# A copy of the centred rows between TensorE and the norm, in the attention layers of a four-layer graph network

## The chip, the cores and the metric

The kernel runs on one core of one Trainium2 chip. The metric is the device time of one execution in microseconds. A profile is one more execution of the same program, recorded by the hardware profiler; its span is the time from its first to its last instruction. Engines are named as in the profile: PE is the matrix engine (PEld its weight loads), DVE the vector engine, ACT the scalar engine, POOL GpSimd, SP the engine that issues most transfers.

## The reference

Input is x, of shape (8, 2048, 128), and a 2048 x 2048 adjacency matrix that is sparse (some 17 neighbours a row). Four layers follow one another: attention, graph, attention, graph. An attention layer is a transformer block whose softmax runs over a node's neighbours alone, with 8 heads of 16; a graph layer has one additive score for each edge. Cut to what matters:

```python
# attention layer (0 and 2)
scores = einsum('bnhd,bmhd->bhnm', h @ Wq, h @ Wk) / sqrt(16)      # by heads
attn = softmax(where(adj == 0, -inf, scores))
x = h + (attn @ (h @ Wv) @ Wo + bo)
x = layer_norm(x) * ln1_g + ln1_b
y = relu(x @ W1 + b1) @ W2 + b2                                    # 128 -> 256 -> 128
x = layer_norm(x + y) * ln2_g + ln2_b
# graph layer (1 and 3)
h = x @ W
e = leaky_relu((h @ a_src)[:, :, None] + (h @ a_dst)[:, None, :], 0.2)
out = softmax(where(adj == 0, -inf, e)) @ h
x = ln_gamma * layer_norm(out + x) + ln_beta
```

The layer norm is (x - mean) / sqrt(variance + 1e-5) over the 128 features. It stands twice in each attention layer and once in each graph layer; the change is in the two of the attention layers.

## The kernel before

**Units.** The 2048 nodes are cut into 32 units of 64. Batches come in two halves of four, so a unit's data is a tile of 128 partitions (64 nodes by two halves) by 4 x 128 columns; transposed it is 128 features by 512. At the start the kernel builds, from the adjacency, the list of neighbour rows that each unit needs (`block_list`, `unit_list`), as nine groups of 128 rows. Building runs alongside layer 0. Each layer then reads a table in HBM that the layer before wrote (`project`, its copies into the tile `trows`).

**An attention unit.** For each unit `attention` takes five steps: four of two groups and one of a single group. A step gathers rows of keys and values by indirect DMA from POOL's queue (`kv<-table,idx`, L1469), PE spreads the queries over them (`qe`, L1542), DVE multiplies (L1554) and reduces over a head's 16 columns (`s`, L1561), ACT takes the exponential (L1571), POOL weighs the values (L1580; for some steps DVE does, from an exponential that ACT puts into a PSUM tile `ps_e`), and PE sums by target node (`acc` and `sums`, L1615). The buffer `kv` exists six times.

**After attention.** `after_attention` takes the sums of a unit: DVE divides (L1633, L1637), PE transposes (`ps_t`), ACT copies to `at`, PE multiplies by Wo (`ps_o`), DVE adds bias and residual into the tile `r` (L1649). Then comes the norm. `centred` multiplies `r` by I - 1/128 on PE, which takes the mean off and turns the rows back, into the PSUM tile `ps_c` (L1310). `norm` reads it twice: four squares with their sum (ACT, L1406, each followed by a read of the accumulator), a root as logarithm and exponential (L1416, L1417), and four scalings by it into `normed` (L1439). `scaled` transposes (`ps_t`, L1298) and applies gain and offset (L1449). Two products with W1, the rectifier into `hidden` (L1669), a product with W2 (`ps_y`, L1679), the second sum into another `r`, and the second norm in the same manner follow; at the end the rows go to HBM (`xd`) and into the next layer's table (L1345 or L1343, L1288, L1383).

**The graph layers** use the same `norm`. There `r` is an SBUF tile that DVE wrote (L1865: `ps_c` plus the weighted sum), so both readings are from SBUF.

**What sets the order.** Every operation is given to a planner with a cost for each engine that may run it, a key, the cells that it reads and writes, and the buffers that it takes. `Plan.order` is a list scheduler: at each moment an engine takes the ready operation of the smallest key whose buffers are free. Its result is the program order of each engine, and each engine then runs in that order. A unit's steps have keys from n x 1000 + 5u on; its exponentials come four earlier and its norm five later. So the exponential of a step goes ahead of the norms when both are ready, but doesn't interrupt one that runs. `either` lets ACT alone run an operation, and ACT or DVE in the last two units of a layer (`late`):

```python
def either(self, scalar, vector):
    return {"ACT": scalar, "DVE": vector} if self.late else {"ACT": scalar}
```

**Buffers that bear on the change.** All small PSUM tiles (`ps_q`, `ps_t`, `ps_o`, `ps_c`, `ps_f`, `ps_y`, `ps_p`, `ps_e`, and those of the list building: `ps_off`, `ps_aux`, `ps_l`) share the tag `m` with two slots. `r` has two buffers in SBUF.

```python
PSUM_BUFS = {"q": 1, "acc": 1, "sums": 1, "m": 2}
```

The functions that the diff touches, with what calls them:

Of the kernel before, what the change touches and what calls it, by code (L numbers as in the profile page):

```python
# [65 lines left out]
class Dense:  # L66
# [181 lines left out]
    def norm(self, out, r, gain, offset):  # L248

        nc = self.nc  # L250
        stats = self.two.tile([P, TB, 6], F32, name="stats")
        mv = self.two.tile([P, TB, 2], F32, name="mv")
        for t in range(TB):
            nc.vector.bn_stats(stats[:, t, :], r[:, t, :])
        for t in range(TB):
            nc.vector.bn_aggr(mv[:, t, :], stats[:, t, :])
        ve = self.two.tile([P, TB], F32, name="ve")
        nc.gpsimd.tensor_scalar(ve, mv[:, :, 1], EPS, None, ALU.add)
        rstd = self.two.tile([P, TB], F32, name="rstd")
        nc.gpsimd.tensor_tensor(rstd, ve, self.neg_half, ALU.pow)  # L260
        xn = self.one.tile([P, TB, P], F32, name="xn")
        for t in range(TB):
            nc.vector.tensor_scalar(
                xn[:, t, :], r[:, t, :], mv[:, t, 0:1], rstd[:, t : t + 1], ALU.subtract, ALU.mult
            )
        nc.gpsimd.tensor_tensor(xn, xn, gain.unsqueeze(1).to_broadcast([P, TB, P]), ALU.mult)
        nc.gpsimd.tensor_tensor(out, xn, offset.unsqueeze(1).to_broadcast([P, TB, P]), ALU.add)
# [146 lines left out]
    def after_attention(self, x, L, c, heads):  # L414

        nc = self.nc
        x = x[:, c * TB : (c + 1) * TB, :]
        ft = self.across(heads)
        ps = self.ps_m.tile([P, CH], F32, name="ps_p", tag="m")
        for t in range(TB):  # L420
            cols = slice(t * P, (t + 1) * P)
            nc.tensor.matmul(ps[:, cols], lhsT=ft[:, cols], rhs=L["Wo"], start=True, stop=True)
        r = self.one.tile([P, TB, P], F32, name="r")
        nc.vector.tensor_tensor(r, ps.rearrange("p (t e) -> p t e", t=TB), x, ALU.add)
        x1 = self.one.tile([P, TB, P], F32, name="x1")
        self.norm(x1, r, L["ln1_g"], L["ln1_b"])
        ft = self.across(x1)
        nc.gpsimd.tensor_tensor(x1, x1, L["b2"].unsqueeze(1).to_broadcast([P, TB, P]), ALU.add)
        hidden = self.one.tile([P, FFN // P, CH], F32, name="hidden")
        for f in range(FFN // P):  # L430
            ps = self.ps_m.tile([P, CH], F32, name="ps_f", tag="m")
            nc.tensor.matmul(ps, lhsT=L["W1"][:, f * P : (f + 1) * P], rhs=ft, start=True, stop=True)
            nc.scalar.activation(hidden[:, f, :], ps, AF.Relu, bias=L["b1"][:, f : f + 1])
        ps = self.ps_m.tile([P, CH], F32, name="ps_y", tag="m")
        for t in range(TB):
            cols = slice(t * P, (t + 1) * P)
            for f in range(FFN // P):
                nc.tensor.matmul(
                    ps[:, cols],
                    lhsT=hidden[:, f, cols],  # L440
                    rhs=L["W2"][:, f, :],
                    start=(f == 0),
                    stop=(f == FFN // P - 1),
                )
        r = self.one.tile([P, TB, P], F32, name="r")
        nc.vector.tensor_tensor(r, ps.rearrange("p (t e) -> p t e", t=TB), x1, ALU.add)
        self.norm(x, r, L["ln2_g"], L["ln2_b"])
# [290 lines left out]
def flat(ap):  # L738
    return ap if len(ap.shape) == 2 else ap.rearrange("p b d -> p (b d)")


class Sparse:
# [585 lines left out]
    def project(self, n, u, x, key, of=None, shares=()):  # L1328
# [66 lines left out]
            {"SP": 0.9}, store, key, reads=[rows], joins=[self.table[n]], dma=P * hb * width * 4  # L1395
        )

    def norm(self, r, key):

        hb = self.HB  # L1400
        var = self.cell("var", [P, hb, 2])

        def squares(e, b):
            x = flat(r.tile)[:, b * P : (b + 1) * P]
            if e is self.nc.scalar:
                e.activation(self.junk, x, AF.Square, scale=P**-0.5, accum_out=var.tile[:, b, 1:2])  # L1406
            else:
                e.bn_stats(self.stats, x)
                e.bn_aggr(var.tile[:, b, :], self.stats)

        for b in range(hb):
            self.op(self.either(0.55, 0.4), lambda e, b=b: squares(e, b), key, reads=[r], joins=[var])
        rstd = self.cell("rstd", [P, hb])

        def root(e):
            e.activation(rstd.tile, var.tile[:, :, 1], AF.Ln, bias=self.eps)  # L1416
            e.activation(rstd.tile, rstd.tile, AF.Exp, scale=-0.5)  # L1417

        self.op({"ACT": 0.5}, root, key - 2, reads=[var], writes=[rstd])
        normed = self.cell("normed", [P, hb, P])  # L1420
        for b in range(hb):
            self.op(
                self.either(0.37, 0.28),
                lambda e, b=b: self.scale(
                    e, normed.tile[:, b, :], flat(r.tile)[:, b * P : (b + 1) * P], rstd.tile[:, b : b + 1]
                ),
                key,
                reads=[r, rstd],
                joins=[normed],
            )  # L1430
        return normed
# [194 lines left out]
    def after_attention(self, n, u, acc, sums, x, base):  # L1626
        self.late = u >= self.NU - 2
        L, hb = self.layers[n], self.HB
        op, cell = self.op, self.cell
        key = base + TG  # L1630
        rc = cell("rc", [P, hb * H])

        op({"DVE": 0.35}, lambda e: e.reciprocal(rc.tile, sums.tile), base, reads=[sums], writes=[rc])  # L1633
        a = cell("rows", [P, hb, P], name="a")

        def divide(e):
            e.tensor_tensor(  # L1637
                a.tile.rearrange("p b (h d) -> p (b h) d", d=HD),
                acc.tile.rearrange("p (c d) -> p c d", d=HD),
                rc.tile.unsqueeze(2).to_broadcast([P, hb * H, HD]),  # L1640
                ALU.mult,
            )

        op({"DVE": 0.65}, divide, base, reads=[acc, rc], writes=[a])

        def add_to(r, ps, bias, other, key):
            op(
                {"DVE": 0.72},
                lambda e: e.scalar_tensor_tensor(r.tile, ps.tile, bias, other.tile, ALU.add, ALU.add),  # L1649
                key,  # L1650
                reads=[ps, other],
                writes=[r],
            )

        at = cell("at", [P, CH])
        ps = self.transposed(a, key, at)
        op(self.either(0.6, 0.68), lambda e, ps=ps: self.copy(e, at.tile, ps.tile), key, reads=[ps], writes=[at])
        r = cell("r", [P, CH], name="r1")
        ps = self.product(L["Wo"], at, key, "ps_o", r)
        add_to(r, ps, L["bo"], x, key - 2)  # L1660
        normed = self.norm(self.centred(r, key), key)
        x1 = self.scaled(normed, L["ln1_g"], L["ln1_b"], "x1", key)
        hidden = cell("hidden", [P, FFN // P, CH])
        for f in range(FFN // P):
            ps = self.product(L["W1"][:, f * P : (f + 1) * P], x1, key, "ps_f", hidden)

            def relu(e, f=f, ps=ps):
                if e is self.nc.scalar:
                    e.activation(hidden.tile[:, f, :], ps.tile, AF.Relu, bias=L["b1"][:, f : f + 1])  # L1669
                else:  # L1670
                    e.tensor_scalar(hidden.tile[:, f, :], ps.tile, L["b1"][:, f : f + 1], 0.0, ALU.add, ALU.max)

            op(self.either(0.7, 0.68), relu, key, reads=[ps], joins=[hidden])
        r = cell("r", [P, CH], name="r2")
        ps = cell("m", [P, CH], name="ps_y")
        for f in range(FFN // P):
            op(
                {"PE": 1.0},
                lambda e, f=f, ps=ps: e.matmul(  # L1679
                    ps.tile,  # L1680
                    lhsT=L["W2"][:, f, :],
                    rhs=hidden.tile[:, f, :],
                    start=(f == 0),
                    stop=(f == FFN // P - 1),
                ),
                key,
                reads=[hidden],
                writes=[ps],
                holds=[r],
            )  # L1690
        add_to(r, ps, L["b2"], x1, key - 2)
        normed = self.norm(self.centred(r, key), key)
        x = self.scaled(normed, L["ln2_g"], L["ln2_b"], "xnew", key)
        self.keep(u, x, key)
        self.project(n + 1, u, x, key)
# [297 lines left out]
```

## Time and profile before

| | us |
|---|---|
| median of three runs | 3263.28 |
| the three runs | 3248.80, 3263.28, 3274.68 |
| the profiled execution | 3296.99 |
| its span | 3295.2 |

| engine | busy us | share of the span |
|---|---|---|
| PE | 2532.1 | 77% |
| DVE | 2311.1 | 70% |
| ACT | 1399.5 | 42% |
| POOL | 2104.5 | 64% |

The stages, by the places in the trace where POOL stops gathering: attention 0 up to about 1190 us (the lists to 850), graph 1 to about 1790, attention 2 to about 2720, graph 3 to the end. The span holds 63,421 instructions and moves 1023 MB, 310 GB/s on the mean, with a granted TensorE clock of 0.867. A share of busy time over the whole span mixes these stages; a stage's own share is read from the table of windows.

A row of a group reads: line, engine, operation, output and inputs by tile, partitions x elements of output and input, count; behind the bar the busy time in us and the mean ns of one; behind the second bar the idle time of the engine just before these instructions, and what ended it. A row of waits reads: who waited, for whom, us in total, times, the longest. A row of the timeline reads: start, duration, engine, line, operation.

### The profile page before, as it was taken

How to read it: one execution, taken by the hardware profiler on the slowest of the kernel's cores; microseconds unless marked ns; L12 is line 12 of the kernel's file. 1: busy time of each engine (PE TensorE's matmuls, PEld its weight loads, DVE VectorE, ACT ScalarE, POOL GpSimd, SP SyncE). 2: the span in 40 equal slices, each digit the busy share in tenths (PEclk: the TensorE clock that was granted, in tenths of full speed). 3: DMA queues.
4: the chain of work that ended last, by engine and by line, in shares of the span. 5: the costliest groups of instructions: out<-in, count | busy, mean ns of one | idle time of the engine just before them, and what ended most of it. 6: DMA issues, size and time to landing. Idle time of an engine off the chain costs nothing. (4 is left out here: it accounts for less than half of the span.)

```text
span 3295.2 us, 63421 instructions
## 1 busy us (share of the span) xinstructions
PE 2532.1 (77%) x23624; PEld 1474.1 (45%) x23624; DVE 2311.1 (70%) x3617; ACT 1399.5 (42%) x4894; POOL 2104.5 (64%) x1447
## 2 busy tenths in 40 slices
PE   6777888878878866788876788888887785777675
PEld 5633444444334334565654233334443343555454
DVE  4789889878878763444444998998989873445554
ACT  4435455555444422444443244444444441333333
POOL 0168777777878835555563777878787835555552
PEclk8769889899999977888898899999999996778877
DMA  7868879887889749999997989999998848899994
GB/s 252 304 228 325 313 285 370 308 337 292 321 321 347 301 156 322 347 327 332 324 352 257 358 331 376 356 353 350 357 354 351 352 186 281 289 317 313 312 302 160
DMA packets 261246, 1023.15 MB, mean 310 GB/s; under 512 B 40193, under 2 KB 69633, under 8 KB 189025
## 3 DMA queue, kind: packets, MB, share of 16 engines
q0 software_dynamic: 166464, 864.44, 70.4%
q1 hardware_dynamic: 94464, 154.56, 13.7%
q8 instruction: 190, 3.11, 0.4%
q14 instruction: 128, 1.04, 0.1%
HBM read 978.59 MB, written 88.08 MB: 324 GB/s over the span
## 5 line engine op out<-in xcount | busy, mean ns | idle before, releaser
L1469 POOL DMA_INDIRECT kv<-table,idx x1152 | 1191.3, 1034 | 931.7 <-issue 395.9
L1580 POOL TENSOR_TENSOR kv<-kv 128x2048 f32<-128x2048 f32 (+1 forms) x252 | 900.0, 3584 | 76.8 <-ACT kv L1571 72.9
L1554 DVE TENSOR_TENSOR kv<-qe,kv 128x2048 f32<-128x2048 f32 (+1 forms) x320 | 662.7, 2071 | 184.6 <-DMA kv<-table,idx 117.2
L1561 DVE TENSOR_REDUCE s<-kv 128x128 f32<-128x2048 f32 (+1 forms) x320 | 659.4, 2061 | 11.4
L1542 PE MATMUL qe<-q_sb,hot 32*128 32x512 f32 (+1 forms) x2304 | 400.2, 700 | 193.7 <-DVE kv L1554 183.5
L1615 PE MATMUL acc<-kv,hot 128*32 128x512 f32 x2560 | 371.4, 658 | 55.1 <-POOL kv L1580 49.6
L1810 DVE TENSOR_TENSOR w<-hot,e 128x512 f32<-128x512 f32 (+1 forms) x384 | 222.2, 597 | 163.6 <-ACT e L1800 83.0
L1825 PE MATMUL acc_q<-kv,w 128*32 128x129 f32 x5120 | 264.7, 314 | 93.7 <-issue 66.7
L1825 PE MATMUL acc<-kv,w 128*32 128x129 f32 x2560 | 155.1, 330 | 135.2 <-issue 89.1
L1825 PEld LDWEIGHTS acc_q<-kv,w 128*32 128x32 f32 x5120 | 177.3, 124 | 166.7 <-issue 117.5
L1542 PEld LDWEIGHTS qe<-q_sb,hot 32*128 32x128 f32 (+1 forms) x2304 | 106.7, 197 | 319.3 <-DVE kv L1554 247.8
L1571 ACT ACTIVATE kv<-s 128x128 f32<-128x128 f32 (+1 forms) x320 | 95.1, 298 | 313.7 <-DVE s L1561 190.8
L1825 PE MATMUL sums<-kv,w 128*32 128x129 f32 x2560 | 171.6, 319 | 58.0 <-issue 57.3
L1406 ACT ACTIVATE junk<-ps_c 128x128 f32<-128x128 f32 x496 | 137.4, 277 | 175.6 <-PE ps_c L1310 116.0
L1288 ACT COPY trows<-ps_p 128x258 f32<-128x258 f32 (+1 forms) x230 | 108.3, 473 | 223.8 <-PE ps_p L1345 90.5
L1615 PEld LDWEIGHTS sums<-kv,hot 128*32 128x32 f32 x2560 | 88.8, 118 | 217.9 <-issue 214.6
L1320 PE MATMUL ps_f<-x,W 128*128 128x512 f32 x256 | 156.8, 700 | 20.5 <-ACT x L1449 12.1
L1825 PEld LDWEIGHTS acc<-kv,w 128*32 128x32 f32 x2560 | 86.4, 127 | 186.4 <-issue 120.0
L1800 ACT ACTIVATE e<-e 128x16 f32<-128x16 f32 (+1 forms) x320 | 65.6, 211 | 219.9 <-DVE e L1795 124.5
L1310 PE MATMUL ps_c<-centre,r 128*128 128x128 f32 x1024 | 145.7, 287 | 14.9 <-DVE r L1649 10.9
L1310 PEld LDWEIGHTS ps_c<-centre,r 128*128 128x128 f32 x1024 | 125.9, 194 | 67.1 <-DVE r L1649 32.3
L1679 PE MATMUL ps_y<-hidden,W 128*128 128x512 f32 x256 | 145.7, 654 | 3.3 <-DVE kv L1580 1.7
(170 smaller groups left out, 4052.4 us busy)
## 6 DMA issues: line engine op xcount, KB each, us to landing
table<-trows SPq DMA_DIRECT2D x128, 256.0 KB
xd<-xnew SPq DMA_DIRECT2D x96, 256.0 KB
x<-xd SPq DMA_DIRECT2D x96, 256.0 KB
kv<-table,idx POOLq DMA_INDIRECT x1152
table<-trows SPq DMA_DIRECT2D x128, 130.0 KB
kv<-adj_dram SPq DMA_DIRECT2D x16, 1024.0 KB
kv<-xt_dram SPq DMA_DIRECT2D x8, 1024.0 KB
x<-xt_dram SPq DMA_DIRECT2D x32, 256.0 KB
```

The costliest lines, as they stand in the source:

```text
L1310: e.matmul(ps.tile[:, cols], lhsT=flat(x.tile)[:, cols], rhs=self.centre, start=True, stop=True)
L1320: lambda e: e.matmul(ps.tile, lhsT=w, rhs=x.tile, start=True, stop=True),
L1406: e.activation(self.junk, x, AF.Square, scale=P**-0.5, accum_out=var.tile[:, b, 1:2])
L1469: e.indirect_dma_start(out=rows(kv.tile, j), out_offset=None, in_=self.tables[n], in_offset=bass.IndirectOffsetOnAxis(ap=self.idx[:, u, co ...
L1542: e.matmul(qe.tile[:, j, hf, :], lhsT=hot.tile[rows, t * P : (t + 1) * P], rhs=q.tile[rows, :], start=True, stop=True,)
L1554: e.tensor_tensor(k, qe.tile[:, 0:tiles].rearrange("p j h c -> p (j h) c"), k, ALU.mult)
L1561: e.tensor_reduce(s.tile[:, 0 : tiles * heads].rearrange("p (q c) -> p q c", q=2 * tiles), k, axis=mybir.AxisListType.X, op=ALU.add,)
L1580: e.tensor_tensor(v, v, w.unsqueeze(3).to_broadcast([P, 2 * tiles, heads // 2, HD]), ALU.mult)
L1615: e.matmul(out[rows, :], lhsT=hot.tile[:, col : col + GROUP], rhs=rhs[:, 2 * (j % tiles) + hf, :], start=(t == 0 and out is acc.tile), sto ...
L1679: lambda e, f=f, ps=ps: e.matmul(ps.tile, lhsT=L["W2"][:, f, :], rhs=hidden.tile[:, f, :], start=(f == 0), stop=(f == FFN // P - 1),),
L1810: e.tensor_tensor(w.tile[:, j : j + tiles], oh[:, j : j + tiles].unsqueeze(2).to_broadcast(shape), e8.tile[:, 0:tiles].unsqueeze(3).to_bro ...
L1825: e.matmul(acc(b)[rows, :], lhsT=w.tile[:, j, hf * hb + b, :], rhs=both_rows(kv)[:, j % tiles, hf * hb + b, 1 : P + 2], start=first and b ...
```

## The change

After the centring product a new operation copies `ps_c` from PSUM into `r`, the SBUF tile that the product has just read. Both readings of the norm then take `r`. The planner is told a cost of 0.6 us on ACT or, in the last two units of a layer, 0.68 us on DVE. The `ps_c` slot ends with the copy; `r` stays taken up to the norm's last scaling. The graph layers keep their code.

```diff
+    def back(self, ps, r, key):
+
+        self.op(self.either(0.6, 0.68), lambda e: self.copy(e, r.tile, ps.tile), key, reads=[ps], writes=[r])
+        return r
+
     def norm(self, r, key):
...
         ps = self.product(L["Wo"], at, key, "ps_o", r)
         add_to(r, ps, L["bo"], x, key - 2)
-        normed = self.norm(self.centred(r, key), key)
+        normed = self.norm(self.back(self.centred(r, key), r, key), key)
         x1 = self.scaled(normed, L["ln1_g"], L["ln1_b"], "x1", key)
...
         add_to(r, ps, L["b2"], x1, key - 2)
-        normed = self.norm(self.centred(r, key), key)
+        normed = self.norm(self.back(self.centred(r, key), r, key), key)
         x = self.scaled(normed, L["ln2_g"], L["ln2_b"], "xnew", key)
```

## The prediction

> **What bounds the kernel now.** I read the page's first and fourth part, then busy time by stage, the groups by shape, the waits, and the timeline of single norms. No engine is full over the whole span, and the engine that the change loads has little of the chain that ended last:
>
> ```profile
> PE 2532.1 (77%) x23624; PEld 1474.1 (45%) x23624; DVE 2311.1 (70%) x3617; ACT 1399.5 (42%) x4894; POOL 2104.5 (64%) x1447
> ...
> PE 13%; DVE 8%; issue 7%; DMA 6%; POOL 5%; another core or an unknown queue 2%; ACT 1%; POOLq 0%; SPq 0%; DVEq 0%; ACTq 0%
> ```
>
> The stage table is what counts: busy microseconds in the order of its header, then clock, DMA share and GB/s. The first two rows are attention layer 0 (while the neighbour lists are built, and after), the third is attention layer 2.
>
> ```profile
> core 0: us, PE busy (x) PEld busy (x) DVE busy (x) ACT busy (x) POOL busy (x), PEclk, DMA share, GB/s
> 230.00:720.00 490.00, 401.01 (x2797) 204.33 (x2793) 437.16 (x544) 244.80 (x825) 376.02 (x203) 0.89 0.85 324
> 720.00:1120.00 400.00, 322.53 (x2337) 153.49 (x2325) 314.55 (x217) 189.11 (x650) 322.37 (x177) 0.94 0.86 324
> ...
> 1800.00:2650.00 850.00, 690.82 (x5106) 322.32 (x5107) 762.06 (x473) 378.99 (x1341) 668.11 (x382) 0.94 0.92 356
> ```
>
> In layer 2 DVE is busy 762/850 = 90% and the DMA engines 92%. POOL's 79% grows by the pause of 0.30 us that its timeline shows before nearly every gather (9 gathers in a unit of some 28 us: 2.7/28 = 10 points). Three resources stand near 90% at once. In layer 0 it is DVE while the lists are built (89%) and POOL afterwards (81% and the pauses). ACT has 45 to 50% everywhere, so the change counts only where ACT comes late for one of the three, or where the PSUM slot it frees lets PE run earlier for one of them.
>
> **The change, part by part.** It adds, in each of 64 units (32 in each attention layer), two ACT copies of 128x512, and moves the reads of four squares and four scalings per norm from PSUM to SBUF. No DMA is added or moved, and SP's and POOL's queues keep their work. The rows that price it (mean ns stands after the comma behind the bar):
>
> ```profile
> L1439 ACT ACTIVATE normed<-ps_c,rstd 128x128 f32<-128x128 f32 x496 | 144.5, 369 | 8.7 <-DVE normed L1441 7.1
> L1406 ACT ACTIVATE junk<-ps_c 128x128 f32<-128x128 f32 x496 | 137.4, 277 | 175.6 <-PE ps_c L1310 116.0 <-DVE stats L1408 21.4 <-PE ps_t L1298 11.0
> ...
> L1439 ACT ACTIVATE normed<-r,rstd 128x128 f32<-128x128 f32 x247 | 79.7, 390 | 1.5 <-issue 0.2
> ...
> L1406 ACT ACTIVATE junk<-r 128x128 f32<-128x128 f32 x247 | 76.4, 309 | 130.8 <-DVE r L1865 115.1 <-issue 9.0 <-DVE w L1810 1.9
> ...
> L1507 ACT COPY q_sb<-ps_q 128x512 f32<-128x512 f32 x64 | 37.3, 583 | 40.5 <-PE ps_q L1503 39.5 <-remote 0.8
> ```
>
> The graph layers run the same norm from SBUF, so both forms are measured. Copy: 583 ns, as the q_sb copy. Squares: 309 against 277 ns, but by the pitch at which they start, 0.425 against 0.40 us, 4 x 0.025 = 0.10 us. Scalings: four in a row take 1.28 us from SBUF (2780.92) and 1.14 from PSUM (2322.40), 0.14 us. Together 0.82 us for each norm, 128 x 0.82 = 105 us of ACT. Over the 1880 us or so of the two layers that lifts ACT from about 47% to 53%.
>
> *What of it is on the path.* The work that hides it is POOL's and DVE's on the neighbour rows: while they work, ACT idles half the time. Without that cover it would cost the 105 us. Where the cover ends shows in one wait. ACT runs its queue in the planned order, and queued behind a copy stand the exponentials of the kv tiles, for which POOL's weighing (or DVE's) waits, and behind that PE's sums and the release of the kv buffer to the next gather.
>
> ```profile
> POOL kv L1580 <- ACT kv L1571: 72.9, 31, 9.3
> ```
>
> 31 waits, all in attention. A norm takes 3.3 us of ACT and a unit has two, 6.6 of some 13 us that ACT is busy in a unit, so about half of the 31 stand behind a norm: 16 x 0.82 = 13 us. The low end is 0 (exponentials have the earlier key), the high end is below, in the first rival. I take 13.
>
> *The copy's own wait* for PE's centring is the one that the first square has today; it moves and isn't added.
>
> *The slot given back.* The centred rows hold one of two PSUM slots from the centring to the last scaling:
>
> ```profile
> 2319.07 1.13 PE L1310 MATMUL ps_c<-centre,r 128*128 128x128 f32 x8 [1.23 <-DVE r L1649]
> ...
> 2322.40 1.14 ACT L1439 ACTIVATE normed<-ps_c,rstd 128x128 f32<-128x128 f32 x4
> ```
>
> That is 2322.40 + 1.14 - 2319.07 = 4.5 us; the same subtraction over all norms between 1900 and 2600 gives 5.9 us on average, and after the change 1.1 + 0.6 us and a wait of 0.6 give 2.3. What PE lost directly to such a slot:
>
> ```profile
> PE ps_aux L1095 <- ACT normed L1439: 9.9, 5, 2.6
> ...
> PE ps_off L1074 <- ACT normed L1439: 5.7, 2, 5.2
> ...
> PE ps_q L1503 <- ACT junk L1406: 3.2, 1, 3.2
> ```
>
> 19 us together. PE idles some 326 us in the three stage rows (1740 - 1414), and DVE's two largest waits for PE, those for qe (38.7 us over the run) and ps_o (26.5), are a fifth of that, so a fifth of the 19 is passed on: -4 us, between 0 and -19. The Trainium skill's page "PSUM — Partial Sum Buffer", in its summary of rules, says to empty PSUM promptly because it is tight; by that rule the freed slot decides, and the time would be the second rival's, where the rows above give a few microseconds. Against the change speaks "VectorE: DVE Perf Modes", whose specifications put ScalarE nearer to PSUM and VectorE nearer to SBUF; by that alone ScalarE's reads should stay in PSUM, and only the longer reads would count, 128 x 0.24 = 31 us of ACT if nothing hid them.
>
> *The layer's end.* In the last two units DVE shares the norm, and from PSUM the two engines take turns:
>
> ```profile
> 2715.83 0.28 ACT L1406 ACTIVATE junk<-ps_c 128x128 f32<-128x128 f32 x1 [0.36 <-DVE stats L1408]
> ...
> 2717.97 0.37 ACT L1439 ACTIVATE normed<-ps_c,rstd 128x128 f32<-128x128 f32 x1 [0.42 <-DVE normed L1441]
> ```
>
> The first read starts at 2714.76 and the last ends at 2718.34: 3.6 us. The last norm of the graph layer, from SBUF, has both engines side by side: 3275.63 to 3278.04, 2.4 us. With a copy of 0.58 to 0.68 and a hand-over of 0.1 that is 3.1 to 3.2, a gain of 0.4 a norm; two in series at each of two ends: -1.6 us. If DVE's work were not shared there, each would cost 0.82 instead, +3.3.
>
> *r held longer.* r, with two buffers, now lives to the last scaling, some 5 us more each. A unit's second r can't start before its first is read out, so two buffers serve two overlapping units: 0, with the price in the third rival if it binds.
>
> **Sum.** +13 - 4 - 1.6 = +7 us. The profiled execution took 3296.99 us (span 3295.2 and 1.8 around it), the slowest of those shown: the median of the three runs is 3263.28, 1.0% lower. On the profiled one the sum is 3304; on the median, which I predict, 3270. The three runs lie 26 us apart, so about 1%, 33 us, is what a measurement of this kernel can tell from no change.
>
> **Rivals.** *First, slower: the copies stand in front of the exponentials.* Place: ACT's order in the loaded stages. Price: 0.82 us for each copy that an exponential must let pass when POOL has no slack; after the lists POOL needs 9 x 1.33 + 4 x 3.70 + 1.0 = 27.8 us a unit, all that a unit takes there. If half of the 128 are passed on whole, 52 us: 3315. It decides from 40 copies on (33/0.82). For it: the 72.9 us of waits, and three resources at 90% with no room to catch up. Against: ACT has 1% of the chain.
>
> *Second, faster: the slot was what ordered the plan.* Both slots are held at once for more than half of layer 2 by the same subtraction for every tile in them, and the centred rows are the largest holder. A full slot seldom shows as a wait, because the planner then puts something else first. DVE's waits for qe, ps_o, ps_t (8.7), ps_y (8.2) and ps_l (31.6 in all layers) make 114 us; if 40% go, -45: 3218. Against: the chain after attention has no user before the next layer, and layer 2 waits for gathers more than for PE.
>
> *Third, the reordering alone.* One more operation shifts all later choices of the list planner, with r bound longer. DVE's share in the seven 100-us stretches of layer 2 from 1900 to 2600 lies between 87 and 92%, 1.1 points from their mean on average; 1.1% of some 1700 us is 19 us either way, 3251 or 3289: within 1%, and part of the forecast's range.
>
> *Fourth, that the copy isn't there or runs on DVE.* Only the last two units of a layer offer DVE as a choice; 8 copies at 0.68 us, 5 us at most: the forecast.
>
> **How the numbers follow.** Forecast with the third and fourth, within 1%: 0.40. First rival, slower by over 1%: 0.34. Second, faster by over 1%: 0.26. The unknown terms run from -19 to +52 us, and the slot from -45: 3218 at the low end. At the top, the first rival and a few of the reordering's microseconds: 3325. That leaves a tenth outside on each side. The likeliest one's own range is 3245 to 3295.
>
> **What would show it.** Right: 126 to 128 new copies of some 0.58 us on ACT; junk from r near 309 ns and scalings near 390; ACT near 52% in layer 2, DVE and DMA still near 90% there; the PE waits on ACT normed for ps_aux and ps_off gone; in the last units squares on ACT and DVE overlapping. Wrong towards slower: POOL's wait for the exponential above 110 us. Wrong towards faster: units in layer 2 under 27.3 us and DVE over 92%. If the time moves by more than 1% with none of these, the plan's order did it.

## The result and the profile after

The changed kernel takes 3280.82 us (median of seven runs, 3271.18 to 3300.93) against 3263.49 us (seven runs, 3248.80 to 3274.68) for the kernel before. The ratio is 1.0055, 95% interval 1.003 to 1.008: 10 to 26 us slower, at 18. On another chip, where the kernel before takes 3058.78 us, the ratio was 1.0101 (1.0067 to 1.0135). The forecast was 3270 us.

The two profiled executions can't be subtracted as they stand: that of before (3296.99 us) lies above all seven of its timed runs, that of after (3271.18) is the fastest of its own. Most of the 26 us between them lies in the graph layers, whose code the change leaves alone: from its first to its last residual sum a graph layer takes 500 and 498 us in the one profile, 486 and 489 in the other. What can be read from one profile is what each engine did.

The stage table of the changed kernel, the same columns and stages as before:

```profile
core 0: us, PE busy (x) PEld busy (x) DVE busy (x) ACT busy (x) POOL busy (x), PEclk, DMA share, GB/s
230.00:720.00 490.00, 388.03 (x2761) 201.07 (x2757) 432.07 (x536) 260.06 (x837) 373.44 (x201) 0.89 0.84 322
720.00:1120.00 400.00, 325.59 (x2304) 156.23 (x2298) 310.52 (x217) 210.83 (x677) 317.04 (x174) 0.92 0.84 318
...
1800.00:2650.00 850.00, 702.32 (x5223) 324.93 (x5219) 767.71 (x482) 426.60 (x1433) 679.19 (x387) 0.95 0.93 362
```

ACT rose from 379 to 427 us in the layer-2 stretch, 45 to 50%. There DVE (767.7 for 762.1) and POOL (679.2 for 668.1) got more done in the same 850 us. In the two layer-0 stretches they got less done: DVE 432.1 for 437.2 and 310.5 for 314.6, POOL 373.4 for 376.0 and 317.0 for 322.4. The two attention layers moved in opposite directions. That is the first sign that no price per copy explains the result, for both layers have the same copies.

The groups by shape, with the new copy:

```profile
L1444 ACT ACTIVATE normed<-r,rstd 128x128 f32<-128x128 f32 x741 | 239.0, 390 | 2.4
L1411 ACT ACTIVATE junk<-r 128x128 f32<-128x128 f32 x740 | 228.1, 308 | 143.9 <-DVE r L1870 110.6 <-issue 11.8 <-DVE w L1815 4.5
...
L1288 ACT COPY r<-ps_c 128x512 f32<-128x512 f32 x127 | 73.7, 581 | 135.0 <-PE ps_c L1310 123.2 <-issue 9.1 <-DVE kv L1585 1.6
```

127 copies ran on ACT (one of the 128 on DVE), 581 ns each; squares take 308 ns and scalings 390, as forecast. The wait for the centring passed from the first square to the copy (116.0 us became 123.2). The waits for the norm's slot are almost gone: of PE's waits on ACT that belong to this slot, the list now has, beside 0.7 us for `ps_t`,

```profile
PE ps_q L1508 <- ACT r L1288: 4.3, 4, 2.1
```

and none for `ps_aux` or `ps_off`. The centred rows hold the slot 2.2 us on average between 1900 and 2600, where it was about 6; both slots are held at once 40% of that time, where it was 56%. POOL's wait for the exponentials is almost what it was (72.9):

```profile
POOL kv L1585 <- ACT kv L1576: 75.6, 34, 7.6
```

### The profile page after: what moved, and what is told of

The parts are those of the page before. It is cut to its first block, busy times and chain, and to the rows that moved or that the text cites. A ratio compares the mean times of both kernels' runs of the same rounds, so it can differ in the third digit from the quotient of the medians.

```text
span 3269.5 us, 63597 instructions
## 1 busy us (share of the span) xinstructions
PE 2516.5 (77%) x23624; PEld 1461.3 (45%) x23624; DVE 2315.0 (71%) x3626; ACT 1488.9 (46%) x5014; POOL 2100.7 (64%) x1446
## 5 line engine op out<-in xcount | busy, mean ns | idle before, releaser
L1830 PE MATMUL acc_q<-kv,w 128*32 128x129 f32 x5120 | 272.3, 317 | 95.6 <-issue 66.6
L1411 ACT ACTIVATE junk<-r 128x128 f32<-128x128 f32 x740 | 228.1, 308 | 143.9 <-DVE r L1870 110.6
L1444 ACT ACTIVATE normed<-r,rstd 128x128 f32<-128x128 f32 x741 | 239.0, 390 | 2.4
```

What stands on the lines that cost most here:

```text
L1444: e.activation(out, in_, AF.Copy, scale=by)
L1830: e.matmul(acc(b)[rows, :], lhsT=w.tile[:, j, hf * hb + b, :], rhs=both_rows(kv)[:, j % tiles, hf * hb + b, 1 : P + 2], start=first and b ...
```

## The experiments

Each kernel was timed 4 to 12 times beside the kernel before on the same chip. The chips differ. The kernel before took 3296.26 us beside four of the kernels: the copies without a new order, the new order without the copies' time, the copies three times, and the slot kept in the plan. It took 3052.34 us beside the two replanned kernels and the two with the copy in one layer, and 3058.78 beside the other four. So ratios are compared, and the microseconds given are the ratio's part of that chip's time. Theory A is the forecast's: the copies' time on ACT is what costs. Theory B: the order that the planner makes anew is what costs. Theory C: every copy is passed on whole. The diffs are cut to what matters; what stands behind a # in them is a note.

### The copies without a new order

The plan of before is kept, and the copy is issued inside the first square's operation, which tells the planner nothing. The programs of PE, POOL and SP are then instruction for instruction those of before.

```diff
+            r = self.cell("cen", [P, CH])          # SBUF, two buffers of its own
...
         def squares(e, b):
+            if b == 0:
+                self.copy(e, r.tile, ps.tile)
```

> The plan of before, instruction for instruction, with the 128 copies put in right ahead of the first square of each norm (into an SBUF buffer of their own), and both readings taking the copy. So this is the copies' time on ACT without any new order. Theory A, the forecast's: the copies delay the exponentials behind them; the whole +18 us of the change is here, against before +10 to +20 us. Theory B, the new order did it: within 6 us of before. Theory C, every copy is passed on because three resources are full: +40 to +60 us.

Measured: ratio 0.9978 (0.9957 to 0.9998), -7 us. With all the copies and the old order the kernel isn't slower; it is a little faster, by about as much as theory B allowed (6 us). Theories A and C fall as the account of the whole, and B is left. This kernel also gives the slot back early, so it doesn't yet say what the copies' time costs by itself; a later kernel does.

### The new order without the copies' time

```diff
-        self.op(self.either(0.6, 0.68), lambda e: self.copy(e, r.tile, ps.tile), key, reads=[ps], writes=[r])
+        self.op(self.either(0.6, 0.68), lambda e: self.copy(e, r.tile[:, 0:1], ps.tile[:, 0:1]), key, reads=[ps], writes=[r])
```

> The order of the changed kernel, with the slot given back early, but each copy moves one column of 512 only, so the norm reads rows that are not centred: the copy's time is left out (some 0.17 us in place of 0.58 on ACT, about 52 us of ACT less). Theory A: it falls back to before or below, -5 to +4 us against before. Theory B: it stays where the changed kernel is, +12 to +24 us against before.

Measured: 1.0043 (1.0022 to 1.0063), +14 us. The copies here take 155 ns, so 54 us less of ACT, and the loss stays within the change's interval:

```profile
L1288 ACT COPY r<-ps_c 128x1 f32<-128x1 f32 x127 | 19.6, 155 | 145.2 <-PE ps_c L1310 133.1 <-issue 8.5 <-PE sums L1620 1.6
```

Together with the last run: the loss follows the order, and not the copies.

### The copies three times over, in the old order

The same kernel as the first, with three copies in place of one.

> As the kernel with the order of before, but each copy is issued three times, so 256 more copies, 150 us more of ACT, ACT some 60% busy in the attention layers. Theory A: the cost grows faster than the dose, +40 to +70 us against before. Theory B: ACT has room even for that, under +20 us. Theory C: three times its price for one copy, +120 us or more.

Measured: 1.0124 (1.0099 to 1.0149), +41 us. ACT has room for one copy and not for three: 256 more copies, 143 us more of ACT in the trace, cost 48 us more than the first kernel. This is theory A's number, and its mechanism shows in POOL's wait for the exponentials, 72.9 us in the kernel before. In the first kernel and in this one it is:

```profile
POOL kv L1589 <- ACT kv L1580: 78.4, 36, 9.5
```
```profile
POOL kv L1589 <- ACT kv L1580: 99.1, 38, 16.1
```

The mechanism is real, but its price at one copy is small.

### The copies made and not read

The old order, the copies issued, and both readings left on PSUM.

```diff
+            if b == 0:
+                self.copy(e, cen.tile, ps.tile)    # cen: written, read by nothing
         x = flat(ps.tile)[:, b * P : (b + 1) * P]  # squares and scalings read PSUM, as before
```

> The order of before and the 128 copies, as in the kernel with the copies' time only, but both readings of the norm stay with PSUM and nothing reads the copy: ACT's time for the copies without the slot given back early and without ACT and DVE side by side in the last units. If the copies' time is hidden and the slot is worth nothing at a fixed order: within 5 us of before. If the -7 us of that kernel is a cost of copying of +4 to +13 us and a gain from the slot of 11 to 20: +4 to +13 us.

Measured: 1.0032 (1.001 to 1.0054), +10 us. This is the price of the copies' time at a fixed order. The forecast's +13 took in the longer readings from SBUF as well, which this kernel doesn't have; for the copies alone its working gives 16 x 0.58 = 9, and that agrees. The first kernel differs from this one only in reading the copy, so in giving the slot back early, in the layers' end, and in the longer readings, which count against it. From 1.0032 to 0.9978 is -0.54%; with both intervals, -0.84 to -0.24%, some 8 to 27 us. The two ran on different chips, so the size is rough.

### The layers' end alone

The first kernel, with the copy in the last two units of each attention layer only (8 of 128).

> The order of before, with copies only in the last two units of each attention layer (8 of 128), where ACT and DVE take turns on PSUM. If the gain of the kernel with the copies' time only is the layers' end: -3 to -7 us against before. The forecast's own estimate for it: -1.6 us, not to be told from none.

Measured: 0.9988 (0.9966 to 1.001), no difference that can be told; the traces say more. From the last division to the first gather of the next layer, at the end of layer 0, it takes 33.8 us in the profile of before and 34.8 where the copies aren't read, but 29.0 in the changed kernel, 28.4 in the first kernel and 28.6 in this one: 5 us less. The other kernels agree, whatever their order: 32.1 to 33.4 us in those four that make no copy in layer 0, 27.6 to 29.1 in those four that make and read one there; with the copies three times over it is 34.1. At the end of layer 2 there is nothing such: 32.5 before, 32.6 after. The alternation that was shown before the change has gone. The last norm of layer 2 in the changed kernel, from the timeline:

```profile
2701.59 0.59 ACT L1288 COPY r<-ps_c 128x512 f32<-128x512 f32 x1 [3.61 <-PE ps_c L1310]
2702.21 0.31 ACT L1411 ACTIVATE junk<-r 128x128 f32<-128x128 f32 x1
...
2702.21 0.29 DVE L1413 BATCH_NORM_STATS2 stats<-r 128x6 f32<-128x128 f32 x1 [1.93 <-ACT r L1288]
...
2703.93 0.70 ACT L1444 ACTIVATE normed<-r,rstd 128x128 f32<-128x128 f32 x2
```

ACT's square and DVE's statistics start together at 2702.21, and the norm takes 2703.93 + 0.70 - 2701.59 = 3.0 us with its copy, 3.6 before without. The Trainium skill's page "PSUM — Partial Sum Buffer", in its part on bank collisions, says that accesses of two engines to one bank have to be kept apart, reads by ScalarE and VectorE included. These traces agree: on PSUM each engine waited for the other, 0.22 to 0.43 us at a turn, and on SBUF they overlap.

### A new order without the copy

The kernel before, with one number told to the planner changed, and nothing computed otherwise. First 1.13 in place of 1.10 us for the centring products:

> The kernel before, no copy; the planner is told 1.13 us in place of 1.10 for the centring products, which changes the order and nothing else (2890 of 52878 positions of PE's program differ, the change itself made 3274 differ). Theory B (the order did it, and order is a lottery of this size): it moves by 5 to 30 us, either way, from before. Theory A: within 6 us of before.

Measured: 1.0132 (1.0114 to 1.015), +40 us, more than was expected of any new order. Then 0.52 in place of 0.55 us for a square:

> As the last, with 0.52 in place of 0.55 us told for a square. Same expectations: theory B, 5 to 30 us away from before, either way and not by the same amount as the other replanned kernel; theory A, within 6 us.

Measured: 1.0044 (1.002 to 1.0068), +13 us. (The counts of positions in the expectation take in the dense fallback program, which doesn't run.) Three hundredths of a microsecond in one planned cost move this kernel nearly as much as the change did, or more: +1.3% and +0.4% against +0.55% on one chip and +1.0% on another. In the second, layer 0 is quicker and layer 2 slower: its last division of layer 0 ends at 1163.2 us, and layer 2 takes 871 us from its first division to its last, where the order of before takes 849 to 854 us on this kind of chip.

### The copy in one layer only

```diff
-        normed = self.norm(self.back(self.centred(r, key), r, key), key)
+        normed = self.norm(self.centred(r, key) if n else self.back(self.centred(r, key), r, key), key)
```

> The changed kernel with the copy in attention layer 0 only. The two profiles put the loss into layer 0 (its divisions span 971 us before and 989 after) and a gain of 11 us into layer 2. If that holds: +14 to +28 us against before. If the layers share the cost: +5 to +12 us.

Measured: 1.0103 (1.0083 to 1.0124), +31 us. The other way round, with the copy in layer 2 only:

> The changed kernel with the copy in attention layer 2 only; layers 0 and 1 have the order of before. If the loss is layer 0's: -12 to +3 us against before. If the layers share the cost: +5 to +12 us.

Measured: 0.9983 (0.9964 to 1.0002), -5 us. The first has the changed kernel's order in layer 0 and that of before in the rest, the second the reverse, each up to its layer's end. The two sum to +0.86%, and the whole change on the same kind of chip gave +1.01%. So the loss is layer 0's, and it is somewhat more than the 14 to 28 us expected of it.

### The changed kernel on another chip

> The changed kernel again, beside the others on one chip, to compare ratios across chips: 1.003 to 1.008 of before as measured. With its order at 1.0043 without the copies' time, the copies' time is +0.0 to +0.3% of that.

Measured: 1.0101 (1.0067 to 1.0135), +31 us. Its interval and that of the first chip overlap only from 1.0067 to 1.008, so the price may differ with the chip; the two measurements don't settle it.

The traces of the kernels with the same order of layer 0 agree across chips, with or without the time of one copy. From the first division of layer 0 to the end of the last:

| order of layer 0 | kernels | us |
|---|---|---|
| of before | before; copies' time only; layer 2 only; copies unread; layers' end | 971, 963, 957, 973, 966: mean 966 |
| of the change | changed; order only; layer 0 only; changed again | 989, 991, 991, 995: mean 991 |

25 us in layer 0 on the mean, and no kernel of one row comes near those of the other; the kernel with three copies, in the order of before, has 984. In layer 2, between the same marks, the slower chips have 859 (before) and 863 (copies' time only) against 848 (changed) and 848 (order only), the quicker ones 849, 851 and 854 against 842, 844 and 850: a gain of 6 to 13 us by the new order.

One row differs in all of these traces in the same manner, POOL's waits between 220 and 1160 us. Of before, of the kernel with the copies' time only, of the changed kernel and of the kernel with the copy in layer 0 only:

```profile
POOL kv L1469 <- PE sums L1615: 25.4, 18, 3.2
```
```profile
POOL kv L1478 <- PE sums L1624: 18.9, 13, 3.0
```
```profile
POOL kv L1474 <- PE sums L1620: 48.2, 25, 3.9
```
```profile
POOL kv L1474 <- PE sums L1620: 55.6, 25, 4.0
```

These are gathers at the head of POOL's queue that wait until PE has summed the last tile out of the kv buffer they will fill. In the old order they cost 19 to 26 us (22.9 to 26.1 in four more kernels), in the new one 48 to 56 (53.5 and 52.5 in two more). Not all of it is loss: POOL's idle time of no shown cause fell from 101.9 to 80.7 us between before and after. By 1160 us POOL has done 729.75 us of work in the changed kernel and 737.45 in the one before, so it is 8 us of work behind. That the new places of the gathers are the cause is argued from this and not shown: no kernel was run in which these alone were moved. The kernel with 0.52 told for a square speaks against it as a rule for all orders. It has more of these waits than the order of before, and still the shortest layer 0 of all, 948 us:

```profile
POOL kv L1469 <- PE sums L1615: 35.6, 18, 6.5
```

What it is in the new order that costs the 25 us stays open.

### The slot kept to the end in the plan

```diff
-        normed = self.norm(self.back(self.centred(r, key), r, key), key)
+        ps = self.centred(r, key)
+        normed = self.norm(self.back(ps, r, key), key, [ps])     # scalings share ps: its slot ends with them
```

> The changed kernel, but the planner counts the PSUM slot as taken up to the last scaling, as before the change, so the plan gains nothing from the copy. Theory A with a gain from the slot: slower than the changed kernel by 4 to 10 us, so +22 to +28 us against before. If the slot is worth nothing to the plan: the same as the changed kernel within 8 us. The second rival of the forecast (the slot orders the plan): +50 us or more against before.

Measured: 1.0146 (1.012 to 1.0171), +48 us: layer 0 takes 1000 us and layer 2 879 between the marks above. It says that the plan did worse without the early slot, but it is one more order, and since two harmless changes of a cost moved the time by 13 and 40 us, this run doesn't price the slot. It is inconclusive.

### The better parts together

The order with 0.52 told for a square in layer 0, and the copy in layer 2 only.

> The order of the replanned kernel with 0.52 in layer 0 (its last division there ends at 1163 us, against 1180 to 1191 with the order of before), and in layers 1 to 3 that of the kernel with the copy in layer 2 only. Theory B, each layer's order counts by itself and the parts add: -12 to -28 us against before, faster than before and than the change. If a layer's order counts only together with the others: within 8 us of before or slower.

Measured: 0.9971 (0.9949 to 0.9993), -9 us, under both kernels (1.0101 for the changed one beside it). It was to be -12 to -28: layer 2 brought what it was to bring (850 us between the marks), but layer 0 ended at 1181.3 in the profiled execution and not at 1163, and took 962 us in place of 948 by the same order. The forecast that the parts add is neither borne out nor refuted by this: a single profile of an order is not good to 15 us.

## Why the prediction was right or wrong

**Right in the result's class and range.** The time stayed within 1%, between 3218 and 3325 us, and went the way that the sum said, with 7 us forecast and 18 measured. On the second kind of chip, +1.0%, the change stands at the forecast's border to slower. That the sign came out is luck: the terms that were in the sum, copies, slot and layers' end, make -7 us together at a fixed order and not +7, and the slowdown came from a term that was put at nothing.

**Right: the price of the copies on ACT.** 581 ns, squares and scalings as the graph layers' rows gave them, 50% of ACT in layer 2 (52 was written). The term for the path was +13 us; at a fixed order the copies alone cost +10 (3 to 17), where the working gives 9. But most of it doesn't show where the working put it: POOL's wait for the exponentials rose by 2.7 us in the changed kernel and by 5.5 in the first, and not by 13.

**Undersized: the slot and the layers' end.** -4 and -1.6 us were in the sum. Reading the copy at a fixed order is worth some 17 us (8 to 27). Of these, 5 lie at the end of layer 0, where the working took 0.4 us for each norm from the length of one norm (measured: 0.5 for the last one) and took it for both ends alike; why it is 5 us at one end and none at the other is not settled. The rest, some 12 us, is not placed. The step that failed is the fifth of 19 us: it counted only waits whose releaser the profile names as the norm, and carried PE's overall slack over to them. PE's waits of this kind are 15 us where the copies aren't read and 7 where they are, so even passed on whole they make 8. The fifth itself was read low: DVE's wait for `ps_l`, 31.6 us, is larger than that for `ps_o`, and with it the share is 97 of 326 us, 30%, or -6 us in place of -4. The rule in the summary of the Trainium skill's page "PSUM — Partial Sum Buffer", to empty PSUM promptly, pointed the right way at a fixed order, where the rows had made the slot small; the -45 us worked out for the rival that follows it is more than twice what was measured.

**Wrong: the order as a term of mean zero.** "1.1% of some 1700 us is 19 us either way" took the spread of stretches within one plan for the spread between plans, and entered the sum as nothing. The plans differ by about as much or more: +14 us for the new order nearly without the copies' time, +40 and +13 for two replannings of the kernel before. By the ratios, the order is what lies between the first kernel and the change, both with all copies read: from 0.9978 to 1.0055, +0.77% or some 25 us, measured on two chips. By the parts, the change is +10 for ACT's time, about -17 for the slot and the end, and +25 in layer 0 with -6 to -13 in layer 2 for the order: +5 to +12 where +18 was measured, which the intervals of these parts cover. The forecast's last sentence named it, "the plan's order did it", for a move over 1%; it held for a smaller one.

**The rivals.** The first, the copies in front of the exponentials, falls at one copy and appears at three (+41 us). The second, the slot, has the right sign at a fixed order and less than half of its price. The third decided the sign, at some 25 us by the ratios where it named 19. The fourth doesn't hold: 127 copies ran on ACT.

## What to carry to other kernels

When an edit goes through a list scheduler, its cost has two parts, and they can be measured apart: issue the new instruction inside an existing operation, so that the order stays, and separately replan with a cost changed by a few hundredths. If the second moves the time as much as the edit did, the edit isn't yet judged by one run of it. A slot given back early can be worth more than the waits that name it; why it was here is not shown.

## What the runs showed of the hardware that was not expected

The same order of the graph layers runs at different rates on different chips, while the attention layers hardly differ. The kernel with the copies' time only, on the chip where the kernel before takes 3296 us, and the kernel with the copies unread, where it takes 3059, each in the stretch from 1300 to 1600 us, which lies in the first graph layer:

```profile
1300.00:1600.00 300.00, 240.83 (x3295) 174.00 (x3288) 128.87 (x475) 129.89 (x464) 165.74 (x160) 0.85 0.93 331
```
```profile
1300.00:1600.00 300.00, 247.06 (x4097) 197.40 (x4097) 161.87 (x588) 165.78 (x580) 202.04 (x195) 0.87 1.03 404
```

331 against 404 GB/s, and 160 against 195 instructions of POOL in the same time; in layer 2, from 1840 to 2570, the two have 354 and 360 GB/s. A graph layer takes 506 and 432 us between its first and its last residual sum. So a ratio measured on one chip weighs the layers differently from another, and the same loss in an attention layer is a larger share on the quicker chip, though by only 8% (3296 to 3059 us), which is not enough to make +1.0% of +0.55%.
